# A sparse graph layer on one core: edge items worked out as a maximum and a minimum over columns sorted by sign

## The chip, the cores and the metric

The kernel runs on one core of one Trainium2 chip. The metric is the device time of one execution in microseconds (us), from the first to the last instruction of that core with what lies around it; lower is better. Engines are called by the profile's letters: PE (TensorE, matrix products), DVE (VectorE), ACT (ScalarE), POOL (GpSimd, which here issues the indirect DMAs) and SP (SyncE, which issues plain DMAs). Each engine works through its own instructions in the order in which they stand in its queue.

## What is computed

A batch of 32 entries of 512 nodes with 256 features goes through four layers on one sparse 512 x 512 matrix `adj`. Layers 0 and 3 are the same kind, layer 1 is a plain graph layer, layer 2 is attention. Cut to what matters here:

```
def gnn(h, adj, W1, b1, W2, b2, Wa, ba, Wm, bm, beta1, beta2, beta3):   # layers 0 and 3
    pre_u = h @ W1[:256];  pre_v = h @ W1[256:]
    hidden = relu(pre_u[:, :, None, :] + pre_v[:, None, :, :] + b1)     # for every pair u, v
    S = sigmoid(hidden @ W2 + b2)                                       # one number for every pair
    a_t = einsum('buv,bud->bvd', S * adj, h)
    m_t = einsum('uv,bud->bvd', adj, h) * h
    return beta1 * h + beta2 * (a_t @ Wa + ba) + beta3 * (m_t @ Wm + bm)
x = gnn(x, adj, L0...)
x = x + relu((adj @ x) @ L1_W.T + L1_b)
x = attention(x, adj, L2...)                                            # softmax over 512 neighbours
x = gnn(x, adj, L3...)
```

`S` is multiplied by `adj`, so it is needed only where `adj` is not zero: at the edges and on the diagonal. `adj` is drawn with about 1.6% of its cells filled, and its diagonal is full.

## The kernel before, in words

`Counts` (L177 on) counts the edges of each row, and one branch on that count chooses between a dense path, not taken here, and a sparse path. The sparse path lists the edges off the diagonal as 36 **items** (`Edges`): 128 edges each, one to a partition; 32 of them are own items (eight for each of the four blocks of 128 rows) and four are **panels**, the overflow of rows with more than eight edges.

The batch is worked in eight groups of four entries, and each group goes through two edge stages, one for layer 0 and one for layer 3: 16 edge stages in all. A stage has three parts.

- `pre` (L582 on) computes, for each of four entries and each of four row blocks, `pre_u` and `pre_v` by PE, adds `b1` to the first (DVE, L596), copies the second (ACT, L597), and writes the pair `puv` to a table in memory through SP (L604; `puv` has three buffers). For the self loops it also adds the two halves and takes relu, times W2, summed (DVE, L599 and L600). That is 256 `puv` pairs in all, three DVE instructions each.
- `edges` (L650 on) goes through the 36 items. For each it gathers 128 rows of 1024 numbers (four entries of 256) by an indirect DMA from POOL (L646, into one of five `rows` tiles), adds the matching tile `mine` (L731), takes relu and multiplies by W2, and sums over the 256 columns. Where the sum is left to ACT, DVE does the product in one instruction of 1024 columns (L739) and ACT sums in four (L717); otherwise DVE does product and sum in four instructions of 256 columns (L747). In 14 stages every second item up to the 31st is of the first kind, 16 of 36; in the first and in the last stage, which have spare row tiles, all 36 are. Every four items a sigmoid follows on a few columns (L614, L618, L619, L675), and POOL scatters each item's 128 x 4 results into a zeroed table of cells (L639).
- `load` reads the filled cells back as the matrix SA (L772), with which PE multiplies.

Between a group's two edge stages lies its **middle stage** (`middle_one`, L876 on): the rest of layer 0, layer 1, the softmax of layer 2 (L958 to L964, and the transposes L1003) and the `pre` of layer 3. `first` makes ready the next group's layer 0, and `last` does layer 3's products.

The order of the work is written by hand: `sparse_path` gives every piece of each of these parts a due time and `weave` issues them in that order. `behind` ties an instruction behind the one that its engine had last got two pieces of the middle stage before, so that the scheduler can't draw it ahead of that. Within these bounds a scheduler with a cost model of its own sets each engine's order at compile time.

Of the kernel before, what the change touches and what calls it, by code (L numbers as in the profile page):

```python
# [34 lines left out]
EARLY = 20  # L35
CELLS = HALF * N
ITEMS = NC * OWN + 2 * PANELS
SPARE = NC // 2 * OWN * P + LINES
GROUP = NB * D
HELD = 12  # L40

# [7 lines left out]
class Model:  # L49


    def __init__(self, ctx, tc, a):
        nc = self.nc = tc.nc
        self.tc, self.a = tc, a
        const = self.const = ctx.enter_context(tc.tile_pool(name="const", bufs=1))
        self.ident = const.tile([P, P], F32, name="ident")
        make_identity(nc, self.ident)
        self.adj = const.tile([P, NC, N], F32, name="adj")
        for c in range(NC):
            nc.sync.dma_start(self.adj[:, c, :], a["adj"][c * P : (c + 1) * P, :])  # L60
        self.g0, self.g3 = self.gnn_first("L0_gnn"), self.gnn_first("L3_gnn")
# [36 lines left out]
    def gnn_first(self, L):  # L98
        nc, a, const = self.nc, self.a, self.const
        w = {"L": L}  # L100
        w["W1"] = self.load(f"{L}_W1", [P, 2 * DC, D], a[f"{L}_W1"].rearrange("(c p) k -> p c k", p=P))
        w["b1bc"] = self.bcast(f"{L}_b1", D)
        w["W2bc"] = const.tile([P, D], F32, name=f"{L}_W2bc")
        nc.scalar.dma_start(w["W2bc"], a[f"{L}_W2"].rearrange("k o -> (k o)").partition_broadcast(P))
        w["b2"] = self.bcast(f"{L}_b2", 1)
        w["nb2"] = const.tile([P, 1], F32, name=f"{L}_nb2")
        w["bcol"] = const.tile([P, DC, 1], F32, name=f"{L}_bcol")
        if L == "L3_gnn":
# [68 lines left out]
class Counts:  # L177
# [3 lines left out]
    def __init__(self, ctx, m):  # L181
# [4 lines left out]
        with tc.tile_pool(name="c_sb", bufs=2) as sb, tc.tile_pool(name="c_ps", bufs=1, space=PSUM) as ps:  # L186
            ones = sb.tile([P, N], F32, name="c_ones", bufs=1)
            nc.vector.memset(ones, 1.0)
            count = sb.tile([P, NC], F32, name="count", bufs=1)
# [17 lines left out]
            nc.vector.tensor_reduce(half, pc.rearrange("p (h c) -> p h c", h=2), AX.X, ALU.add)  # L207
            most = sb.tile([1, 1], F32, name="most")
            nc.vector.tensor_reduce(most, half, AX.X, ALU.max)
            nc.vector.tensor_scalar(self.excess, most, float(-LINES), None, ALU.add)  # L210
# [193 lines left out]
class Group:  # L404
# [3 lines left out]
    def __init__(self, sp, w, name):  # L408
# [7 lines left out]
        self.self_s = sp.grp.tile([P, NC, NB], F32, name=f"self_s{name[0]}")  # L416

# [5 lines left out]
class Sparse:  # L423
# [3 lines left out]
    def __init__(self, ctx, m, counts, xr, outr, B):  # L427
# [16 lines left out]
        self.act, self.small, self.gath = pool("act", 1), pool("small", 2), pool("gath", 5)  # L444
# [78 lines left out]
    def big(self, dtype, n, layer=None):  # L523

        self.bigs += 1
        if layer is None:
            layer = 3 if self.bigs <= NC else 0
        return self.act.tile([P, n], dtype, name="big", tag=f"SA{layer}", bufs=NC)

    def setup(self):  # L530


        for w in (self.m.g0, self.m.g3):
            self.nc.vector.tensor_scalar(w["nb2"], w["b2"], -1.0, None, ALU.mult)
        self.zero = self.act.tile([P, GROUP], F32, name="zero", tag="hWa3")
# [30 lines left out]
    def setup_rest(self):  # L566
        yield from self.rest

# [13 lines left out]
    def pre(self, g, b, hT):  # L582
# [3 lines left out]
        for c in range(NC):  # L586
            cs = slice(c * P, (c + 1) * P)
            if c % 2 == 0:
# [7 lines left out]
            nc.vector.tensor_tensor(puv[:, 0, :], pp[:, 0:D], w["b1bc"], ALU.add)  # L596
            nc.scalar.copy(puv[:, 1, :], pp[:, D:])  # L597
            both = self.small.tile([P, D], F32, name="both", bufs=1)
            nc.vector.tensor_tensor(both, pp[:, D:], puv[:, 0, :], ALU.add)  # L599
            nc.vector.scalar_tensor_tensor(  # L600
                both, both, 0.0, w["W2bc"], ALU.max, ALU.mult, accum_out=g.self_s[:, c, b : b + 1]
            )
# [47 lines left out]
    def edges(self, g, spare=(), own_tags=()):  # L650
# [8 lines left out]
        tags = [None] * 5 + list(spare)  # L659
# [3 lines left out]
        def own_1():  # L663
            self.sigmoid_of(own)
            diag = self.counts.diag.unsqueeze(2).to_broadcast([P, NC, NB])
            nc.vector.tensor_tensor(g.self_s, g.self_s, diag, ALU.mult)
            for q in range(2):
                diagonal = g.cells[q][q * HALF : q * HALF + HALF * (N + 1), :]
                diagonal = diagonal.rearrange("(c p a) b -> p c a b", p=P, a=N + 1)[:, :, 0, :]
                self.written(g, q, nc.sync.dma_start(diagonal, g.self_s[:, 2 * q : 2 * q + 2, :]))  # L670
# [9 lines left out]
        panels = [j for j in e.order if j >= NC * OWN][: len(own_tags)]  # L680

        def fetch(n):
# [4 lines left out]
            j = e.order[n]  # L687
            c = -j if -j in mine and j >= NC * OWN else j // OWN
# [13 lines left out]
            self.fetch(rows, g, e.iv[:, j : j + 1])  # L702
# [10 lines left out]
        def sums(k, rows):  # L713

            for b in range(NB):
                part = rows[:, b * D : (b + 1) * D]
                self.behind(nc.scalar.activation(part, part, AF.Identity, accum_out=g.s[:, k, b : b + 1]))  # L717
# [7 lines left out]
        todo = [(2, lambda: self.exp_of(w, own)), (4, own_1)]  # L725
        done = 0
        for k in range(ITEMS):
            for _ in range(2 if spare and len(ready) > 2 else 1):
                put()
            rows, other = fetched.pop(k)  # L730
            self.behind(nc.vector.tensor_tensor(rows, rows, other, ALU.add))  # L731
            if k + lead < ITEMS:
                fetch(k + lead)
            if summed:
                summed.pop(0)()
            if spare or k % 2 == 1 and k < ITEMS - 3:
                by_entry = rows.rearrange("p (b d) -> p b d", b=NB)
                w2 = w["W2bc"].unsqueeze(1).to_broadcast([P, NB, D])
                nc.vector.scalar_tensor_tensor(by_entry, by_entry, 0.0, w2, ALU.max, ALU.mult)  # L739
                summed.append(lambda k=k, rows=rows: sums(k, rows))  # L740
                if spare:
                    summed.pop(0)()
            else:
                for b in range(NB):
                    part = rows[:, b * D : (b + 1) * D]
                    at = g.s[:, k, b : b + 1]
                    nc.vector.scalar_tensor_tensor(part, part, 0.0, w["W2bc"], ALU.max, ALU.mult, accum_out=at)  # L747
            if k % 4 == 3 or k >= ITEMS - 3:
                ks = slice(done, k + 1)
                near = spare or k >= ITEMS - 5  # L750
                todo.append((k + (1 if near else 3), lambda ks=ks: self.exp_of(w, g.s[:, ks, :].rearrange(flat))))
# [698 lines left out]
```

## Time and profile before

| | |
|---|---|
| median of three runs | 2982.51 us (2976.23 to 2991.17) |
| the profiled execution, its own time | 2998.45 us |
| its span, first to last instruction | 2996.8 us |
| mean clock granted to PE | 0.959 |
| PE busy | 2690.0 us, 90% |
| DVE busy | 2307.1 us, 77% |
| ACT busy | 1336.8 us, 45% |
| POOL busy | 1555.3 us, 52% |
| DMA | 677.30 MB, mean 226 GB/s |

The span is taken in a profiled execution; the 1.65 us between it and that execution's own time lies around the instructions. Busy time is what the profile shows of an engine's instructions. A PE that is shown busy isn't necessarily at its peak, and the idle time of an engine that is not the bottleneck costs nothing.

### The profile page before, as it was taken

To read this page: it belongs to the slowest core of one execution; us is meant where nothing else is said; L and a number is where in the kernel's file an instruction comes from. 1 tells how busy PE (TensorE), PEld (TensorE's weight loads), DVE (VectorE), ACT (ScalarE), POOL (GpSimd) and SP (SyncE) were. 2 spreads that over 40 slices of the span, in tenths; PEclk is the share of its full clock that TensorE was granted. 3 is DMA by queue.
4 is the path that set the end of the run, shared out by engine and by line. 5 is a ranking of instruction groups with operands and counts; after the bars stand their busy time and mean duration, and the time that the engine had idled before them with its cause. 6 is when DMAs were issued, how large, how long until landed. Compare 5 with 4: busy or idle time off the path is not lost. (4 is left out here: it accounts for less than half of the span.)

```text
span 2996.8 us, 32453 instructions
## 1 busy us (share of the span) xinstructions
PE 2690.0 (90%) x8645; PEld 1613.9 (54%) x8646; DVE 2307.1 (77%) x6035; ACT 1336.8 (45%) x4101; POOL 1555.3 (52%) x1328
## 2 busy tenths in 40 slices
PE   6367787989998999989999899989999899988998
PEld 3134344545664566546664466646565466644666
DVE  6874786889588885988778885888858896783494
ACT  3553454445344443544344443445434453453262
POOL 2662463646445673556536464466735564361183
PEclk9678998999999999999999999999999999999999
DMA  8875657796678867787677866687677866663474
GB/s 268 286 225 169 213 174 221 233 300 203 217 217 269 268 211 227 230 262 254 209 222 247 275 207 230 216 268 253 211 228 236 303 227 197 208 211 102 148 244 150
DMA packets 302143, 677.30 MB, mean 226 GB/s; under 512 B 52608, under 2 KB 170880, under 8 KB 293760
## 3 DMA queue, kind: packets, MB, share of 16 engines
q0 software_dynamic: 122688, 414.40, 42.9%
q1 hardware_dynamic: 160304, 223.52, 23.0%
q10 hardware_dynamic: 18960, 37.24, 3.4%
q8 instruction: 70, 1.15, 0.2%
q14 instruction: 121, 0.99, 0.1%
HBM read 529.02 MB, written 146.01 MB: 225 GB/s over the span
## 5 line engine op out<-in xcount | busy, mean ns | idle before, releaser
L646 POOL DMA_INDIRECT rows<-table,iv x552 | 679.0, 1230 | 795.5 <-DMA table<-puv 262.7
L639 POOL DMA_INDIRECT cells<-s,cell x576 | 697.6, 1211 | 420.6 <-DVE s L675 243.2
L731 DVE TENSOR_TENSOR rows<-rows,mine 128x1024 f32<-128x1024 f32 x552 | 666.4, 1215 | 101.4 <-DMA rows<-table,iv 72.8
L717 ACT ACTIVATE rows<-rows 128x256 f32<-128x256 f32 x1088 | 439.6, 406 | 445.4 <-DVE rows L739 396.6
L46 PE MATMUL pst<-adj,h 128*128 128x512 f32 x1024 | 452.2, 592 | 0.0
L747 DVE SCALAR_TENSOR_TENSOR rows<-rows,L_gnn_W2bc 128x256 f32<-128x256 f32 x1120 | 414.0, 417 | 1.6
L739 DVE SCALAR_TENSOR_TENSOR rows<-rows,L_gnn_W2bc 128x1024 f32<-128x1024 f32 x272 | 329.4, 1213 | 0.4
L46 PEld LDWEIGHTS pst<-adj,h 128*128 128x128 f32 x1024 | 192.8, 190 | 219.9 <-issue 217.6
L46 PE MATMUL pst<-L_gnn_Wa,hT 128*128 128x256 f32 x1024 | 248.8, 393 | 62.9 <-DMA hT<-xT 57.8
L46 PEld LDWEIGHTS pst<-L_gnn_Wa,hT 128*128 128x128 f32 x1024 | 198.9, 199 | 103.0 <-issue 59.2
L46 PE MATMUL pst<-eT,feats 128*128 128x512 f32 x512 | 237.7, 619 | 10.9 <-ACT eT L1004 10.9
L46 PE MATMUL pst<-adjT,zW 128*128 128x512 f32 x512 | 228.2, 599 | 11.6 <-ACT zW L916 9.7
L596 DVE TENSOR_TENSOR puv<-pst,bc_L_gnn_b 128x256 f32<-128x256 f32 x256 | 104.9, 416 | 162.4 <-DMA table<-puv 89.2
L597 ACT COPY puv<-pst 128x256 f32<-128x256 f32 x256 | 93.2, 371 | 288.1 <-DVE puv L596 225.9
L1061 PE MATMUL pst<-hWa,SA 128*128 128x256 f32 x896 | 220.3, 400 | 0.0
L1061 PEld LDWEIGHTS pst<-hWa,SA 128*128 128x128 f32 x896 | 213.8, 328 | 3.7 <-issue 1.7
L717 ACT ACTIVATION_READ_ACCUMULATOR rows<-rows 128x1 f32 x1088 | 204.7, 188 | 0.0
L860 ACT COPY flat<-SA 128x512 f32<-128x512 f32 x128 | 136.7, 1128 | 136.6 <-issue 62.9
L891 PE MATMUL pst<-flat,hWa 128*128 128x512 f32 x448 | 196.8, 592 | 0.0
L592 PE MATMUL pst<-w_L_gnn_W,hT 128*128 128x512 f32 x256 | 141.5, 681 | 53.9 <-ACT hT L579 36.5
L46 PEld LDWEIGHTS pst<-eT,feats 128*128 128x128 f32 x512 | 99.9, 198 | 133.2 <-issue 113.3
L46 PEld LDWEIGHTS pst<-adjT,zW 128*128 128x128 f32 x512 | 96.5, 191 | 133.4 <-issue 114.0
(176 smaller groups left out, 3984.2 us busy)
## 6 DMA issues: line engine op xcount, KB each, us to landing
table<-puv SPq DMA_DIRECT2D x256, 256.0 KB
SA<-cells POOLq DMA_DIRECT2D x64, 1024.0 KB
h<-in_x_dram SPq DMA_DIRECT2D x64, 512.0 KB
mine<-table SPq DMA_DIRECT2D x64, 512.0 KB
hT<-xT SPq DMA_DIRECT2D x36, 512.0 KB
xT<-hT ACTq DMA_DIRECT2D x32, 512.0 KB
x2T<-yT SPq DMA_DIRECT2D x32, 512.0 KB
x2s<-x ACTq DMA_DIRECT2D x64, 256.0 KB
```

Source lines behind the costliest of these rows:

```text
L46: nc.tensor.matmul(out, lhsT, rhs, start=(n == 0), stop=(n == len(pairs) - 1))
L592: nc.tensor.matmul(pp, hT[:, 0, ks], w["W1"][:, 0::DC, :], start=True, stop=False)
L596: nc.vector.tensor_tensor(puv[:, 0, :], pp[:, 0:D], w["b1bc"], ALU.add)
L639: ins = self.nc.gpsimd.indirect_dma_start(out=g.cells[half], out_offset=bass.IndirectOffsetOnAxis(ap=at, axis=0), in_=s, in_offset=None)
L646: self.nc.gpsimd.indirect_dma_start(out=rows, out_offset=None, in_=g.table, in_offset=bass.IndirectOffsetOnAxis(ap=at, axis=0))
L717: self.behind(nc.scalar.activation(part, part, AF.Identity, accum_out=g.s[:, k, b : b + 1]))
L731: self.behind(nc.vector.tensor_tensor(rows, rows, other, ALU.add))
L739: nc.vector.scalar_tensor_tensor(by_entry, by_entry, 0.0, w2, ALU.max, ALU.mult)
L747: nc.vector.scalar_tensor_tensor(part, part, 0.0, w["W2bc"], ALU.max, ALU.mult, accum_out=at)
L860: self.nc.scalar.copy(flat[:, r, :], SA[r][:, :, b])
L891: nc.tensor.matmul(pz, hWa[:, r, cs], flat[:, r, :], start=(r == 0), stop=False)
L1061: self.nc.tensor.matmul(pz[:, k * D : (k + 1) * D], SA[r][:, cs, b], hWa[:, r, :], start=(r + k == 0), stop=(alone and k == 1 and r == NC ...
```

## The change

**The arithmetic of an item.** A positive w times relu(u+v) is max(wv, -wu) + wu, and for a negative w it is min(wv, -wu) + wu. So the 256 columns are sorted by the sign of W2: 112 columns that are surely positive (maximum), 112 surely negative (minimum), and the remaining 32 in the old way (add, relu, times W2). The table then holds -w times u and w times v in the sorted columns, an item's DVE work is a maximum of 4 x 112 columns, a minimum of 4 x 112, an add of 4 x 32 and relu times W2 on 4 x 32, and the term that is missing is the sum of u over its 224 columns. That sum, `less`, is made where `puv` is made, and subtracted from an item's 128 x 4 results ahead of the sigmoid. A panel, whose `mine` is gathered row by row, subtracts `mine` itself: one more instruction of 4 x 224 columns. Where DVE makes the sum, it does so with one reduction of 4 x 256 columns in place of four sums of 256.

**Sorting on chip.** `ranks`, in `Counts`, finds each column's place and scale; the excess that the branch reads now also covers the number of positive columns (the dense path is taken if it is below 112 or above 144). `sorted_W1` multiplies W1 by that permutation with PE, for layer 0 ahead of everything else in the sparse path and for layer 3 later. b1 and W2 come in as columns, and their broadcasts are made by PE.

**Self loops as items.** The instructions L599 and L600 in `pre` go. Each edge stage has 40 steps in place of 36: when a row block's first item has had its turn, the block's self loops follow, fetched by a plain DMA from SP, with their sum always on ACT.

**Order and buffers.** The maximum, the minimum and the add of an item are each put `behind` the middle stage, where it was its one add; relu times W2 and the sum follow them by their data. There are six row tiles in place of five. EARLY, the step at which the panels' own rows are fetched in the last stage, is 24 in place of 20.

The diff, cut to its core:

```diff
-EARLY = 20
+EARLY = 24
+STEPS = ITEMS + NC
+SURE = 112
+MIXED = D - 2 * SURE
+PLACE = {0: 0, 2: 1, 1: 2, 3: 3}
...
-        self.act, self.small, self.gath = pool("act", 1), pool("small", 2), pool("gath", 5)
+        self.act, self.small, self.gath = pool("act", 1), pool("small", 2), pool("gath", 6)
...
+    def sorted_W1(self, w):
+        nc = self.nc
+        t = self.big(F32, 2048, 0)
+        W1T = t[:, 0 : 2 * N].rearrange("p (c d) -> p c d", c=DC)
+        by_v, by_u = (t[:, k * N : (k + 1) * N].rearrange("p (c d) -> p c d", c=DC) for k in (2, 3))
+        for to, scale in ((by_u, w["su"]), (by_v, w["sv"])):
+            for c in range(DC):
+                nc.vector.tensor_scalar(
+                    to[:, c, :], self.m.upto_D, w["place"][:, c, :], scale[:, c, :], ALU.is_equal, ALU.mult
+                )
+        for c in range(DC):
+            pt = self.psum()
+            for r in range(2 * DC):
+                nc.tensor.transpose(pt[:, r * P : (r + 1) * P], w["W1"][:, r, c * P : (c + 1) * P], self.m.ident)
+            nc.scalar.copy(W1T[:, c, :], pt)
+        for k, to in enumerate((by_u, by_v)):
+            pp = self.psum()
+            for d in range(DC):
+                rs = slice((DC * k + d) * P, (DC * k + d + 1) * P)
+                mm(nc, pp[:, d * D : (d + 1) * D], [(W1T[:, c, rs], to[:, c, :]) for c in range(DC)])
+            nc.scalar.copy(w["W1"][:, DC * k : DC * (k + 1), :], by_two(pp))
...
-            nc.vector.tensor_tensor(puv[:, 0, :], pp[:, 0:D], w["b1bc"], ALU.add)
+            sure = slice(0, 2 * SURE)
+            less = g.less[:, PLACE[c], b : b + 1]
+            nc.vector.scalar_tensor_tensor(
+                puv[:, 0, sure], pp[:, sure], 1.0, w["b1bc"][:, sure], ALU.mult, ALU.add, accum_out=less
+            )
+            nc.vector.tensor_tensor(puv[:, 0, 2 * SURE :], pp[:, 2 * SURE : D], w["b1bc"][:, 2 * SURE :], ALU.add)
             nc.scalar.copy(puv[:, 1, :], pp[:, D:])
-            both = self.small.tile([P, D], F32, name="both", bufs=1)
-            nc.vector.tensor_tensor(both, pp[:, D:], puv[:, 0, :], ALU.add)
-            nc.vector.scalar_tensor_tensor(
-                both, both, 0.0, w["W2bc"], ALU.max, ALU.mult, accum_out=g.self_s[:, c, b : b + 1]
-            )
...
-            self.fetch(rows, g, e.iv[:, j : j + 1])
+            if k < 0:
+                nc.sync.dma_start(rows, places[c, 1])
+            else:
+                self.fetch(rows, g, e.iv[:, j : j + 1])
...
-            rows, other = fetched.pop(k)
-            self.behind(nc.vector.tensor_tensor(rows, rows, other, ALU.add))
+            rows, other = (t.rearrange("p (b d) -> p b d", b=NB) for t in fetched.pop(n))
+            ups, downs, mixed = (slice(0, SURE), slice(SURE, 2 * SURE), slice(2 * SURE, D))
+            self.behind(nc.vector.tensor_tensor(rows[:, :, ups], rows[:, :, ups], other[:, :, ups], ALU.max))
...
-            if spare or k % 2 == 1 and k < ITEMS - 3:
-                by_entry = rows.rearrange("p (b d) -> p b d", b=NB)
-                w2 = w["W2bc"].unsqueeze(1).to_broadcast([P, NB, D])
-                nc.vector.scalar_tensor_tensor(by_entry, by_entry, 0.0, w2, ALU.max, ALU.mult)
-                summed.append(lambda k=k, rows=rows: sums(k, rows))
+            for cols, op in ((downs, ALU.min), (mixed, ALU.add)):
+                self.behind(nc.vector.tensor_tensor(rows[:, :, cols], rows[:, :, cols], other[:, :, cols], op))
+            nc.vector.scalar_tensor_tensor(rows[:, :, mixed], rows[:, :, mixed], 0.0, w2, ALU.max, ALU.mult)
+            if k >= 0 and e.order[k] >= NC * OWN:
+                sure = slice(0, 2 * SURE)
+                nc.vector.tensor_tensor(rows[:, :, sure], rows[:, :, sure], other[:, :, sure], ALU.subtract)
+            to = g.s[:, k, :] if k >= 0 else g.self_s[:, PLACE[-1 - k], :]
+            if spare or k < 0 or k % 2 == 1 and k < ITEMS - 3:
+                line = rows.rearrange("p b d -> p (b d)")
+                summed.append(lambda to=to, line=line: sums(to, line))
...
             else:
-                for b in range(NB):
-                    part = rows[:, b * D : (b + 1) * D]
-                    at = g.s[:, k, b : b + 1]
-                    nc.vector.scalar_tensor_tensor(part, part, 0.0, w["W2bc"], ALU.max, ALU.mult, accum_out=at)
+                nc.vector.tensor_reduce(to, rows, AX.X, ALU.add)
```

## The prediction

> **What bounds the kernel now.** I read the page's busy shares and slices first, then the busy time by windows, then PE's waits, then the timeline where it idles.
>
> ```profile
> PE 2690.0 (90%) x8645; PEld 1613.9 (54%) x8646; DVE 2307.1 (77%) x6035; ACT 1336.8 (45%) x4101; POOL 1555.3 (52%) x1328
> PE   6367787989998999989999899989999899988998
> DVE  6874786889588885988778885888858896783494
> ```
>
> PE bounds nearly all of it; only what shortens its idle time (2996.8 - 2690.0 = 307 us) counts. By windows it idles 154 us before 500, 125 between 500 and 2700, 27 behind. The columns below are window, length, busy PE, PEld, DVE, ACT, POOL, then PE's clock, DMA share and GB/s.
>
> ```profile
> 125.00:150.00 25.00, 0.40 (x1) 0.00 (x0) 25.00 (x60) 11.54 (x55) 18.49 (x14) 0.61 0.75 238
> 1250.00:1300.00 50.00, 44.36 (x133) 23.36 (x132) 44.06 (x122) 21.53 (x75) 34.74 (x29) 0.97 0.77 244
> 1300.00:1350.00 50.00, 39.89 (x115) 19.46 (x114) 40.27 (x136) 22.16 (x57) 24.84 (x24) 0.97 0.83 276
> 1450.00:1500.00 50.00, 50.00 (x183) 34.91 (x182) 30.98 (x95) 18.48 (x41) 25.44 (x24) 1.00 0.62 212
> ```
>
> In the first edge stage PE starves while DVE is full. Later a group takes some 350 us, with PE full in the second half and 15 to 20 us short around one softmax. PE's waits from 500 to 2700 (total, times, longest):
>
> ```profile
> PE pst L1003 <- DVE ex L964: 37.4, 22, 7.3
> PE pst L592 <- ACT hT L579: 24.0, 6, 4.9
> PE pst L46 <- ACT zW L916: 9.7, 7, 3.2
> PE pst L934 <- DVE yT L923: 8.8, 10, 1.6
> ```
>
> All those on DVE come to 77 us, on ACT to 43. But part of DVE's lateness is a DMA's: in the softmax at 1304 DVE stands in its queue behind a `puv` whose buffer is still being written out:
>
> ```profile
> 1304.43 0.42 DVE L596 TENSOR_TENSOR puv<-pst,bc_L_gnn_b 128x256 f32<-128x256 f32 x1 [2.21 <-DMA table<-puv]
> ...
> 1312.17 0.42 DVE L596 TENSOR_TENSOR puv<-pst,bc_L_gnn_b 128x256 f32<-128x256 f32 x1 [3.40 <-DMA table<-puv]
> ```
>
> **DVE's prices.** From start to start in the timeline:
>
> ```profile
> 2841.13 2.35 DVE L731 TENSOR_TENSOR rows<-rows,mine 128x1024 f32<-128x1024 f32 x2
> 2843.40 2.35 DVE L739 SCALAR_TENSOR_TENSOR rows<-rows,L_gnn_W2bc 128x1024 f32<-128x1024 f32 x2
> ...
> 1256.64 0.42 DVE L747 SCALAR_TENSOR_TENSOR rows<-rows,L_gnn_W2bc 128x256 f32<-128x256 f32 x1
> 1256.98 0.08 DVE L747 DVE_READ_ACCUMULATOR rows<-rows,L_gnn_W2bc 128x1 f32 x1
> 1256.98 0.42 DVE L747 SCALAR_TENSOR_TENSOR rows<-rows,L_gnn_W2bc 128x256 f32<-128x256 f32 x1
> ```
>
> 1024 columns cost 2.27 / 2 = 1.135 us, 256 cost 0.34, the read of the accumulator nothing. So (1.135 - 0.34) / 768 = 1.035 ns a column and 0.075 us an instruction: 448 columns 0.54, 128 0.21, 896 1.00, 224 0.31, 32 0.11.
>
> Item with ACT's sum: before 2 x 1.135 = 2.27, after 2 x 0.54 + 2 x 0.21 = 1.50; there were 296 (rows L739: 272 + 24): -228 us.
> Item summed on DVE: before 1.135 + 4 x 0.34 = 2.50, after 1.50 and a reduction of 1024. The trace has no such reduction; between one pass (1.135) and four of 256 (1.36) I take the first, one instruction with the same columns: 2.64, times 280 (1120 / 4): +38, with the other end +102.
> Panels, 64 subtractions of 896: +64. Self loops, 64 items of 1.50: +96.
> `puv`: before 3 x 0.34 = 1.02, after 0.31 + 0.11 = 0.42, times 256: -154.
> `less`: by the changed program's order 176 subtractions of at most 16 columns at 0.09: +16.
> `ranks` and two `sorted_W1`: some 40 small ones, +7.
>
> Together -161 us of 2307. So the items themselves save next to nothing (-30); what is saved is the self loops' work in `pre`. Here the Trainium skill speaks against the change: "VectorE: DVE Perf Modes", "The DRAIN you can't avoid" and "Rules for kernel authors", says that every DVE instruction pays a pipeline flush before the next, and to keep their count small; the same page puts the fixed term near 150 cycles. The change has 874 more DVE instructions in the program's order. At 150 cycles (an estimate from that page, 0.156 us) they would cost 71 us more than at my 0.075, and the saving would shrink to 90. The spacing of 0.34 us in the rows decides: I keep -161. A dependent pair side by side may add some 0.1 us; the new order mostly interleaves two items, so I take nothing, with 40 us as the bound.
>
> **The other engines.** ACT sums 64 more items, four at 0.40 us (start to start, L717): +102 us, 7% of its load. POOL's count stays, since self loops come by SP. SP gets 64 more loads of 512 KB, 34 MB or 5% of the traffic, and each must wait for a free row tile with table writes, h and hT loads queued behind it. The sixth row tile and EARLY I cost at zero: POOL waits for a tile some 0.4 us a fetch (L646 on L717 and L747, 208 us over 552), mostly beside PE's work; if anything a gain of a few us, and none of a loss. Putting minimum and add `behind` costs nothing where the add was there already; by these prices the changed order has 65 us of edge work between first and last softmax steps, over all 32 entries, where it had 58.
>
> **Where it lands, stage by stage.**
>
> (a) Setup. PE's adj transposes start at 16.56 and the first `pre` at 24.76. Now the branch waits for the ranks (some 30 more small DVE instructions in a chain through PE, and the second W2 column, fifth in ACT's DMA queue): 4 us. Then PE's queue puts W1's transposes and products ahead of adj, and ACT, behind its three DMA issues and a table load of 1.28, must copy four times 0.58 between them: 7 us more. From the first `pre` to 85 the phase also waits on DMAs (3.7 and 5.9 us on table<-puv), which run on meanwhile, so half of the 11 is absorbed: +6 (0 to +12).
>
> (b) First edge stage, 90 to 232, no PE work to hide it. DVE is never idle from 113 to 182, and everything else (puv writes, hence hT loads, hence PE) hangs behind it. It loses 36 x 0.77 - 4 x 1.0 - 4 x 1.5 = 18 us, and of the next group's `pre` 12 x 0.60 = 7. Next late are POOL (some 80 indirect DMAs at about 1.3 + 0.3 us, 128 of 142) and DMA (share 0.75 above), so I take 60%: -15 (-28 to 0).
>
> (c) 225 to 500: PE waits 37 us on DVE; -5.
>
> (d) 500 to 2700. Of DVE's 77 us I put 35 down to the DMA wait shown above (5.9 of the 6 us that one softmax loses). The remaining 42 shrink with DVE's queue: in that softmax the order shows 3.8 us less of other work (six `puv` at -0.60). I take -23, and +5 for the longer ACT queue (12% of its 43): -18 (-50 to +15).
>
> (e) The last stage. PE is busy with held-back products until 2958, then waits 5 us for SA and closes with 28 us of products. Shorter items end sooner, but only 10 us of gaps are there to be closed: -4 (-12 to +3).
>
> Sum: 6 - 15 - 5 - 18 - 4 = -36. The profiled execution took 2998.45, so 2962; its median stands at 2982.51 / 2998.45 = 0.9947 of that: **2947**. Half a per cent, the least that a measurement here can tell from no change, is 15 us; the forecast is past it.
>
> **The rivals.**
>
> *More is freed* (2900). If the DVE waits go almost whole (c -15, d -50), b gives -25 and e -10, and setup its +6, it is -94: 2904 of its own, or 2889; with a little less 2900. For it speaks a rule: "SBUF — State Buffer", "Who interferes with whom", says that a DVE instruction with two SBUF inputs blocks a GpSimd one that reads SBUF. The trace half agrees:
>
> ```profile
> 153.20 1.99 POOL L646 DMA_INDIRECT rows_more<-table,iv  x1 [1.16 <-ACT rows_more L717]
> 166.90 0.94 POOL L646 DMA_INDIRECT rows<-table,iv  x1 [0.30 <-issue]
> ```
>
> The first began just behind an L739 (153.16) and took about that instruction's remainder longer; the second began beside an L731 (166.87) and took no longer. By the rule DVE pieces of 0.54 and 0.21 in place of 1.135 would spare each indirect DMA some 0.15 us, 12 us in (b); by the second row nothing. The forecast takes nothing.
>
> *Hidden* (2982). DVE's saving falls where PE is full, and (b) meets DMA and POOL at once; setup eats the rest.
>
> *Slower: SP's queue* (3018). From 500 to 2700 SP waited 198 us for its 56 loads of `mine` (L692), 3.5 us each, since their tile had to come free. If the 64 self-loop loads wait alike, SP stands 224 us more with table writes behind it; those hold `puv`'s three buffers, DVE's queue stands behind the next `puv` as at 1304 and 1312, and PE behind that. A quarter of it exposed is +56; with 20 left of the gains, 3034 of its own: 3018. It decides once DVE's waits on table<-puv (89 us in all now) grow by more than the 36 gained.
>
> *The dense path* would be far slower, but of W2's 256 numbers, as the reference draws them, 133 are positive, the same in both layers, between 112 and 144. One in a hundred, in the last case.
>
> **How the numbers follow.** Forecast 0.50 (its own range 2915 to 2967), more 0.13, hidden 0.15, slower 0.22. Faster by over 0.5% (below 2967.6): 0.63; within: 0.15; slower: 0.22. The range leaves out about half of the more and of the slower case: 2890 to 3020.
>
> **What would show it.** DVE busy near 2146 and ACT near 1440; PE busy still about 2690; an item on DVE in pieces of 0.54 and 0.21; the first `pre` near 35; SA's first load (L772, at 229 before) near 220; PE's waits for L964 below 30 us between 500 and 2700. Wrong if pieces of 448 columns take over 0.6, if the reduction takes over 1.4, or if SP's new loads are followed by DVE waits on table<-puv.

## The result, and the profile after

The kernel after takes **3005.23 us** (median of 13 runs, 2994.54 to 3025.59), the kernel before 2983.67 beside it (13 runs, 2976.23 to 2999.01): ratio 1.0073, 95% interval 1.0052 to 1.0095. It is 22 us slower, clear of the noise; 2947, which is faster, was forecast. The profiled execution of after took 3000.39 us of its own time (span 2998.7, mean granted clock 0.956).

Busy time and the slices of PE and DVE, from the page of after:

```profile
PE 2694.2 (90%) x8720; PEld 1627.5 (54%) x8720; DVE 2115.5 (71%) x5789; ACT 1439.9 (48%) x4621; POOL 1437.3 (48%) x1332
PE   6647878989998999989999899989999899979968
DVE  6753776778587885878678785878777785763562
```

DVE lost 192 us of work, ACT gained 103, PE has nearly the same to do (2694 for 2690). PE's last slice but one had 9 tenths and has 6: the last stage has a hole. Pieces of items that take turns in DVE's timeline of after (start, length):

```profile
920.57 0.63 DVE L862 TENSOR_TENSOR rows<-rows,mine 128x448 f32<-128x448 f32 x1 [0.36 <-issue]
921.11 1.21 DVE L880 TENSOR_REDUCE s<-rows 128x4 f32<-128x1024 f32 x1
922.24 0.81 DVE L868 TENSOR_TENSOR rows<-rows,mine 128x448 f32<-128x448 f32 x2
922.98 1.08 DVE L872 TENSOR_TENSOR rows<-rows,mine 128x896 f32<-128x896 f32 x1
923.98 0.28 DVE L869 SCALAR_TENSOR_TENSOR rows<-rows,L_gnn_W2bc 128x128 f32<-128x128 f32 x1
```

From start to start it is 0.54 for the maximum, 1.13 for the reduction, 0.74 for minimum and add, 1.00 for the panel's subtraction: the prices forecast. PE's waits from 500 to 2700 in after (total, times, longest):

```profile
PE pst L682 <- ACT hT L669: 29.3, 11, 6.4
PE pst L1142 <- DVE ex L1103: 26.9, 16, 8.3
PE pst L684 <- DVE yT L1120: 24.0, 4, 7.7
PE pst L684 <- ACT hT L669: 9.8, 8, 1.3
```

The softmax's wait (L1142 on L1103, in before L1003 on L964) fell from 37.4 to 26.9, below the 30 forecast. The first, third and fourth rows are the projections of `pre`. With all their releasers PE waits 70.8 us at these two lines, where it waited 46.6 in before (and 48.9 in a second trace of before). All of PE's waits in this stretch come to 124.7 us, and to 124.9 in before: the softmax's waits shrank and the projections' grew. The windows from 500 to 2700 (length, then PE, PEld, DVE, ACT, POOL, clock, DMA share, GB/s), in before and then in after, show the same. The clock in them, 0.98 twice, is 0.983 and 0.978 to three places:

```profile
500.00:2700.00 2200.00, 2074.72 (x6733) 1241.99 (x6733) 1797.66 (x4867) 997.43 (x2986) 1216.22 (x1021) 0.98 0.73 235
500.00:2700.00 2200.00, 2076.54 (x6745) 1248.25 (x6746) 1664.88 (x4449) 1073.53 (x3367) 1135.07 (x1027) 0.98 0.76 248
```

The longest gaps of PE at the projections are 2.9 to 7.7 us in after and 3.6 to 4.9 in before. Two of about 6 us lie near 930 and 970, where one stage meets the next. DVE's timeline of after at the first, and SP's ahead of it:

```profile
930.36 0.15 DVE L1102 RECIPROCAL cols<-cols 128x1 f32<-128x1 f32 x1
934.95 0.39 DVE L688 SCALAR_TENSOR_TENSOR puv<-pst,L_gnn_b1bc 128x224 f32<-128x224 f32 x1 [4.43 <-DMA table<-puv]
935.26 0.08 DVE L688 DVE_READ_ACCUMULATOR puv<-pst,L_gnn_b1bc 128x1 f32 x1
935.26 0.48 DVE L1103 TENSOR_SCALAR ex<-ex,cols 128x512 f32<-128x512 f32 x1
```

```profile
919.38 0.34 SPq L1147 DMA_DIRECT2D h<-x2s  x1
919.94 0.40 SPq L1010 DMA_DIRECT2D hT<-xT  x1
920.49 18.90 SPq L694 DMA_DIRECT2D table<-puv  x5
```

DVE stands for 4.43 us at a `puv` whose buffer is still being written out, and the softmax's L1103 comes behind it. SP had issued that write at 920.49, just behind the loads of h and hT; it took 14.5 us until the buffer was free. A panel's own rows stand in POOL's queue meanwhile:

```profile
931.25 0.94 POOL L736 DMA_INDIRECT rows<-table,iv  x1 [2.22 <-DMA cells<-s,cell]
946.11 0.94 POOL L736 DMA_INDIRECT mine<-table,iu  x1 [13.92 <-DVE rows L872]
```

The tile comes free only with the subtraction of an earlier panel, which stands in that same DVE queue.

The last stage, in after and then in before:

```profile
2850.00:2900.00 50.00, 34.16 (x114) 23.31 (x112) 30.23 (x87) 30.32 (x138) 34.73 (x33) 0.90 0.70 226
2900.00:2950.00 50.00, 37.44 (x113) 24.18 (x114) 28.05 (x70) 16.85 (x73) 22.82 (x22) 0.83 0.66 218
2896.50:2913.60 17.10, 6.45 (x14) 4.71 (x15) 11.45 (x28) 9.21 (x42) 11.54 (x10) 0.50 0.85 235
```

```profile
2850.00:2900.00 50.00, 49.90 (x179) 36.55 (x177) 48.34 (x62) 33.46 (x152) 40.00 (x30) 1.00 0.72 242
2900.00:2950.00 50.00, 42.05 (x133) 27.82 (x134) 43.17 (x60) 27.61 (x122) 39.93 (x31) 0.90 0.62 203
```

Here DVE was busy 48 and 43 of 50 us in before and is idle 20 us of each 50 in after, and PE idles with it. (The third row of after is the stretch at half clock, taken up at the end.) PE's waits of after behind 2785:

```profile
PE pst L1212 <- DVE big L940: 16.6, 4, 13.4
PE pst L51 <- DMA hT<-x2T: 6.8, 3, 3.2
PE pst L1200 <- ACT hWa L930: 5.8, 1, 5.8
```

The 13.4 us are a wait for one product of DVE (L940) while PE's last product before it ended at 2892.3. DVE's timeline shows what the product stood behind:

```profile
2896.22 0.65 DVE L862 TENSOR_TENSOR rows<-rows,mine 128x448 f32<-128x448 f32 x1 [2.23 <-DMA rows<-table,iv]
2901.66 0.62 DVE L862 TENSOR_TENSOR rows_more<-rows_more,mine_more 128x448 f32<-128x448 f32 x1 [3.83 <-issue]
2904.96 0.68 DVE L940 TENSOR_TENSOR big<-pst,hT 128x512 f32<-128x512 f32 x1
```

Edge items stood ahead of it in DVE's queue, and DVE waited 2.23 us for gathered rows of one and 3.83 us at another, for which the trace names no releaser.

Marks along the traces (SP's store of x2 of entry 31, start of the last load of SA, end of the last instruction): before 2809.8, 2959.0, 2992.2; after 2790.3, 2938.0, 2994.6. After enters the last stage 19.5 us ahead and loads the last weights 21 ahead. In before the held-back products are done by then and 33 us of products follow; in after 57 us follow, since PE is still at the held-back ones. From the first mark to the last, PE does the same 597 products in both: busy 170.3 of 204.3 us in after and 168.0 of 182.4 in before. So the last stage is 22 us longer, and 20 of them are idle time of PE.

### The profile page after: what moved, and what is told of

It is laid out like the page before. It is cut to its first block, busy times and chain, and to the rows that moved or that the text cites. A ratio compares the mean times of both kernels' runs of the same rounds, so it can differ in the third digit from the quotient of the medians.

```text
span 2998.7 us, 33271 instructions
## 1 busy us (share of the span) xinstructions
PE 2694.2 (90%) x8720; PEld 1627.5 (54%) x8720; DVE 2115.5 (71%) x5789; ACT 1439.9 (48%) x4621; POOL 1437.3 (48%) x1332
## 3 DMA queue, kind: packets, MB, share of 16 engines
q0 software_dynamic: 122688, 414.40, 42.3%
q1 hardware_dynamic: 169520, 257.08, 25.8%
## 4 chain that ended last, share of the span: by engine, by line
PE 41%; DVE 27%; DMA 18%; issue 7%; ACT 4%; POOL 2%; ACTq 0%; SPq 0%; another core or an unknown queue 0%; DVEq 0%; POOLq 0%
PE pst L51 18%; DMA table<-puv 7%; DMA rows<-table,iv 6%; DVE rows L868 6%; DVE rows L862 5%; PE pst L1200 5%; DVE s L880 4%; PE pst L684 4%; PE pst L682 3%; PE pst L1030 3%; PE pst L1051 2%; PE pst L1073 2%; DVE rows L869 2%; PE pst L1212 2%; ACT rows L846 2%
## 5 line engine op out<-in xcount | busy, mean ns | idle before, releaser
L736 POOL DMA_INDIRECT rows<-table,iv x558 | 638.3, 1144 | 872.6 <-ACT rows L846 238.1
L729 POOL DMA_INDIRECT cells<-s,cell x576 | 643.2, 1117 | 283.9 <-issue 135.6
L846 ACT ACTIVATE rows<-rows 128x256 f32<-128x256 f32 x1344 | 541.9, 406 | 395.4 <-DVE rows L869 366.9
L868 DVE TENSOR_TENSOR rows<-rows,mine 128x448 f32<-128x448 f32 x1232 | 514.4, 445 | 0.0
L862 DVE TENSOR_TENSOR rows<-rows,mine 128x448 f32<-128x448 f32 x616 | 379.9, 617 | 120.9 <-DMA rows<-table,iv 92.8
L880 DVE TENSOR_REDUCE s<-rows 128x4 f32<-128x1024 f32 x280 | 338.1, 1207 | 2.4
L688 DVE SCALAR_TENSOR_TENSOR puv<-pst,L_gnn_b1bc 128x224 f32<-128x224 f32 x256 | 98.8, 386 | 237.3 <-DMA table<-puv 138.7
L846 ACT ACTIVATION_READ_ACCUMULATOR rows<-rows 128x1 f32 x1344 | 253.5, 189 | 4.2 <-issue 4.2
L51 PE MATMUL pst<-eT,feats 128*128 128x512 f32 x512 | 230.9, 605 | 10.7 <-ACT eT L1143 9.3
L692 ACT COPY puv<-pst 128x256 f32<-128x256 f32 x256 | 93.1, 370 | 273.6 <-DVE puv L691 168.4
L1200 PEld LDWEIGHTS pst<-hWa,SA 128*128 128x128 f32 x896 | 214.4, 328 | 10.9 <-ACT hWa L930 6.9
L682 PE MATMUL pst<-w_L_gnn_W,hT 128*128 128x512 f32 x256 | 135.4, 655 | 49.0 <-ACT hT L669 36.6
L869 DVE SCALAR_TENSOR_TENSOR rows<-rows,L_gnn_W2bc 128x128 f32<-128x128 f32 x616 | 175.4, 285 | 2.0
```

The source lines that it names most:

```text
L51: nc.tensor.matmul(out, lhsT, rhs, start=(n == 0), stop=(n == len(pairs) - 1))
L682: nc.tensor.matmul(pp, hT[:, 0, ks], w["W1"][:, 0::DC, :], start=True, stop=False)
L729: ins = self.nc.gpsimd.indirect_dma_start(out=g.cells[half], out_offset=bass.IndirectOffsetOnAxis(ap=at, axis=0), in_=s, in_offset=None)
L736: self.nc.gpsimd.indirect_dma_start(out=rows, out_offset=None, in_=g.table, in_offset=bass.IndirectOffsetOnAxis(ap=at, axis=0))
L862: self.behind(nc.vector.tensor_tensor(rows[:, :, ups], rows[:, :, ups], other[:, :, ups], ALU.max))
L868: self.behind(nc.vector.tensor_tensor(rows[:, :, cols], rows[:, :, cols], other[:, :, cols], op))
```

## The experiments

The theory that most of the runs test: what SP must wait for sets the time. It stands in the edges' loads of own rows (`mine`, L818, and the self loops', L829), table writes and the loads of h and hT come behind, and a lighter DVE meets the late write sooner. The rivals: the self loops as work; the ties; the sixth tile; `puv`'s three buffers by themselves; the panels' tile; the order of the last stage. SP's waits for a line are summed over all rows of its waits. Each ratio is to the kernel before, timed beside that run; after's own is 1.0073.

**A second trace of before** (no edit).

> The kernel before, unchanged, for a second trace of it. The first trace of before came from an execution of 2998.45 us, 15 above its median, that of after from one of 3000.39, 5 below its median, so the two traces differ by 2 us where the medians differ by 21.6. Expected: about 2984 us. If the 15 us that this execution is shorter lie before the last stage (x2 of entry 31 at about 2794 in place of 2809), the lead of 19.5 us that the first pair of traces gave after at that point is mostly an accident of one execution, and after never gained in the middle. If they lie behind it, the lead is real and all of the loss is in the last stage.

Measured 3004.91 us, where the other twelve runs of before on that chip had a median of 2996.09. x2 of entry 31 is stored at 2812.4, and the last instruction ends at 2998.7. So both traces of before are of executions 15 and 9 us above their medians, and after's is of one 5 below. Before's last stage takes 182 and 186 us, after's 204. Of the 21.6 us between the medians the last stage is then some 20. If the 15 and 5 us by which the first two executions are off their medians lie ahead of it, the lead of 19.5 us in the middle is about nothing in a typical execution (2810 - 15 against 2790 + 5). This run was to settle that; it came out long too, so it settles only the last stage.

**The self loops' rows on POOL's queue.**

```diff
-                nc.sync.dma_start(rows, places[c, 1])
+                nc.gpsimd.dma_start(rows, places[c, 1])
```

> After, with the self loops' rows fetched by POOL's queue in place of SP's. Theory of SP's queue: in after SP waits 195 us in these fetches for a row tile to come free, and what is queued behind (the table writes, the loads of h and hT) is late; without that DVE's waits for a table write that frees a puv buffer fall from 128 to about 75 us, the last stage's loads come earlier, and the time falls by 15 to 25 us against after, to about 2985 (ratio to before 1.00). Theory that the last stage's DVE and ACT order is what is late: within 5 us of after (3000 to 3010, ratio 1.006).

Ratio 1.0074 (1.0046 to 1.0102): no change from after, so not the 15 to 25 us that the theory gave. SP's longest waits in these loads, in after and then in this kernel:

```profile
SPq L829 <- DMA rows<-table,iv: 95.1, 6, 16.6
SPq L829 <- DVE s L880: 57.9, 18, 5.3
SPq L818 <- DVE s L787: 49.8, 6, 12.4
```

```profile
SPq L818 <- DVE rows L869: 143.4, 13, 25.4
SPq L818 <- DVE s L787: 80.8, 12, 12.5
```

In after L829 and L818 hold SP 268 and 127 us; with L829 gone L818 holds it 292. SP was not freed, it stands at the next load.

**No self loops among the items.**

```diff
-STEPS = ITEMS + NC
+STEPS = ITEMS
...
-                seq.append(-1 - c)
```

The diff is cut: EARLY is 20 again too, and the diagonal's weights are left out.

> After, with no self loop among the items: 36 steps a group as before, no loads of own rows for them; the diagonal's weights are left out (the sigmoid is taken of the correction alone). It prices the self loops as items with everything that they bring: DVE -96 us, ACT -72, 34 MB of loads, SP's waits. If they carry the loss (by SP's queue, by DVE or by ACT) the time falls by 25 us or more, to 2980 or below (ratio under 0.999). If the loss lies in the ordering of the items or in six row tiles, it falls by under 10 us (ratio 1.004 or more).

Ratio 1.0096 (1.0069 to 1.0123). DVE's busy time falls to 2038.2 us, ACT's to 1335.8, and the time doesn't. The work of the self loops is not the loss, nor is DVE's load what bounds. (Its trace is of the fastest of five executions, 2996.61 us at a median of 3020.48.)

**Ties on the maximum alone.**

```diff
-                self.behind(nc.vector.tensor_tensor(rows[:, :, cols], rows[:, :, cols], other[:, :, cols], op))
+                nc.vector.tensor_tensor(rows[:, :, cols], rows[:, :, cols], other[:, :, cols], op)
```

> After, with only the maximum of an item ordered behind the middle stage, as the addition was before; the minimum and the mixed columns' addition are free to be placed. If the added ties cost (DVE made to wait for work that could have been done earlier) the time falls by 10 us or more, ratio below 1.004. If they cost nothing, or protect the middle stage, it is within 5 us of after or above it (ratio 1.006 or more).

Ratio 1.1384 (1.1355 to 1.1413), clock 0.92. Its group of minima and adds (count, busy and mean ns, idle before and its releasers):

```profile
L868 DVE TENSOR_TENSOR rows<-rows,mine 128x448 f32<-128x448 f32 x1232 | 529.0, 451 | 640.7 <-DMA rows<-table,iv 491.1 <-DMA mine<-table,iu 94.5 <-DMA rows<-table 21.9
```

Untied, the scheduler puts the minima and adds ahead, where their rows haven't come, and DVE stands 641 us at them, 586 of them for gathers. Against after's ratio the ties are worth some 390 us, and without them the split item could not be used.

**Five row tiles; five `puv` buffers, or four tiles of own rows, in the room of the sixth.** All three have five tiles in turn:

```diff
-pool("gath", 6)
+pool("gath", 5)
-        tags = [None] * 6 + list(spare)
+        tags = [None] * 5 + list(spare)
```

with `bufs=5` in place of 3 for `puv` in the second, and `bufs=4` in place of 3 for `mine` in the third.

> After, with five row tiles in turn as before in place of six. One part undone. If the sixth tile only gives the fetches more room, taking it away costs 5 to 15 us (ratio 1.010 to 1.013). If it lets DVE run further ahead of the middle stage into waits that hold up the middle stage's own work, the time falls by 5 us or more (ratio below 1.006).

> After, with five row tiles and, in the room of the sixth, five puv buffers in place of three. Theory of head-of-line waits: where a stage begins, DVE reaches the bias addition into puv 4 to 9 us before the table write that frees its buffer, the softmax steps of the middle stage stand behind it, PE idles 6 us and its clock falls to half for 3 to 10 us; eight such places. With five buffers DVE's waits for table writes fall from 126 us (550 to 2700) to under 30, PE's long gaps at those places vanish, mean clock rises to 0.960 or more, and the time falls by 30 to 60 us against five tiles alone (ratio under 0.995). Theory that these waits only stand in for another bound (the writes themselves, or PE's own work): within 10 us of five tiles alone.

> After, with five row tiles and, in the room of the sixth, four tiles for own rows in place of three. In after SP stands in the own rows' loads while the tile is still read (14 us in one place, with a store of x2T and the table writes behind it), and POOL's fetch of a panel's own rows waits 80 us for the subtraction that frees the tile. If that queueing is the loss, the time falls by 15 us or more against five tiles alone (ratio about 1.000), and DVE's waits for table writes fall below 90 us. If the puv buffers are, it is within 8 us of five tiles alone.

Ratios 1.0197 (1.0173 to 1.0220), 1.0095 (1.0064 to 1.0126) and 1.0182 (1.0161 to 1.0204). The sixth tile saves 1.2%, 37 us, well over the 5 to 15 expected: DVE's waits for rows from 550 to 2700 are 54 us with six and 107 with five. DVE's waits with five tiles, then with five `puv` buffers too:

```profile
DVE rows L862 <- DMA rows<-table,iv: 107.1, 44, 6.4
DVE puv L688 <- DMA table<-puv: 89.2, 27, 9.6
```

```profile
DVE rows L862 <- DMA rows<-table,iv: 111.0, 56, 6.4
DVE puv L688 <- DMA table<-puv: 5.4, 8, 1.5
```

The waits for table writes vanish and the time falls 1.0%, some 30 us, the low end of what was expected. But the ratio was to be under 0.995 and the clock 0.960, and they are 1.0095 and 0.956: these waits cost, and they are not all. PE's longest waits at x2 (L684) stay (7.2 and then 7.4 us at most). Five buffers together with the sixth tile were not run. More tiles of own rows give nothing that can be told: 0.15%.

**Both loads of own rows on POOL's queue**, L818 and L829:

> After, with both loads of own rows (the items' shared tile and the self loop's) on POOL's queue in place of SP's, so that SP never waits for an edge's tile. Theory of SP's queue: ratio to before at or below 1.000, DVE's waits for table writes down from 126 to under 80 us. Theory of the puv buffers alone, or of POOL being held up just as long: ratio 1.005 or more.

Ratio **0.9964** (0.9947 to 0.9982): slightly faster than before. A second time:

> Both own-row loads on POOL's queue, a second time. If the first ratio of 0.9964 holds, 0.995 to 0.998; if it was a lucky call, as the two kernels built on it suggest, 0.998 to 1.000.

Ratio 0.9980 (0.9963 to 0.9996). DVE's waits for table writes (126 us in after), first and second time:

```profile
DVE puv L688 <- DMA table<-puv: 87.8, 22, 5.8
```

```profile
DVE puv L688 <- DMA table<-puv: 64.5, 18, 6.5
```

(In the second another 36 us at `puv` have no releaser shown.)

The mean clock over the timed executions is 0.959 and 0.958 (before beside them 0.959 both times), in after 0.955. The last stage takes 194 us both times.

So the edit gives back the loss, twice. But the traces do not bear out the reason that was behind it. Between 550 and 2700 SP issued after's 193 table writes a median of 0.03 us after both halves of their `puv` were done, 0.8 us at most and 10 us in all: it was not late with them. (For the loads of h and hT the trace doesn't tell it as plainly.) What grew is the time that a write takes. In the waits for which DVE stood, it was on average 8.3 us from SP's issue to DVE's start in after (14.8 at most), 6.9 in before (9.5), and 6.9 and 7.0 with both loads moved (9.5 and 12.3). The edit also takes 67 MB off the DMA queue that SP's transfers share (q1, 257.08 to 189.96 MB) and puts them on that of the gathers (q0, 414.40 to 481.52). Sharing that queue is a rival to SP's standing that no run here separates from it.

**The items' shared own rows alone on POOL's queue, in after and in before**: L818, and its counterpart L692.

> After, with only the items' shared own rows loaded by POOL's queue in place of SP's; the self loops' rows stay on SP. The self loops' rows alone on POOL changed nothing (ratio 1.0074 against after's 1.0073), both together gave 0.9964. If the shared rows' load alone is what held SP, this gives 0.996 to 0.999; if both must go, since either one leaves SP standing, it stays at 1.004 or more.

> The kernel before, with the items' shared own rows loaded by POOL's queue in place of SP's: the control for the last edit. SP stood 235 to 244 us in that load in before, 128 in after. If the load held SP just as much in before, it gains as much here (ratio 0.990 or less), and moving it says nothing of why after is slower. If it is a cost of after alone, the ratio is within 0.997 to 1.003.

Ratios 1.0141 (1.0112 to 1.0171) and 1.0049 (1.0036 to 1.0062). With L818 moved in after, L829 alone holds SP 320 us. So SP's standing in the two falls from 395 us to 292 or 320 with one load moved, and only moving both gives a gain. Moving L818 alone even costs 0.7% against after, which is not explained: PE's waits from 500 to 2700 rise from 125 to 149 us, while DVE's for table writes fall to 103. In before, SP stood 244 us in L692 and moving it off costs half a per cent; the gain isn't one that before could have had.

**Without self loops, own rows on POOL's queue.** The two edits above together.

> After with no self loops among the items (the diagonal's weights left out), and the items' shared own rows on POOL's queue: SP never stands in an edge's load. Without the self loops SP stood 244 us in that load, as much as in before (243), and the ratio was 1.0096. If SP's queue is the cause here too, the ratio falls to 0.996 or less. If the loss without self loops is another (the split item, the panels' tile), it stays at 1.004 or more, as moving this load cost before 0.005.

Ratio 0.9995 (0.9974 to 1.0015), against 1.0096 with the load on SP: again 1%, short of the 0.996 expected. But it isn't by way of `puv`; DVE's waits for table writes are 105.5 us without the move and with it

```profile
DVE puv L688 <- DMA table<-puv: 118.4, 29, 8.5
```

**The panels' tile freed early**, in after, and with both loads moved. The panels' missing term is left out, since columns of `adj` are subtracted in its place:

```diff
-                nc.vector.tensor_tensor(rows[:, :, sure], rows[:, :, sure], other[:, :, sure], ALU.subtract)
+                nc.vector.tensor_tensor(rows[:, :, sure], rows[:, :, sure], self.m.adj[:, :, sure], ALU.subtract)
```

> After, with the panels' subtraction reading the adjacency's first 224 columns in place of the panel's own rows: the same instruction at the same length, but the own rows' tile comes free one instruction group earlier (the panels' weights come out wrong by this). POOL stands up to 13.9 us (seven times, 80 us) in the fetch of a panel's own rows for this subtraction, the rows' fetches queue behind it, DVE waits for them 4 to 7 us at the end of each stage with the last of x2 behind it, and PE idles 5 to 7 us there. If the added subtraction is what makes this, POOL's wait at that line falls to the 5 us of before, PE's waits for x2 at the next projection (24 us) fall below 8, and the time falls by 20 us or more (ratio 1.000 or less). If the fetch is late for other reasons, within 8 us of after (ratio 1.005 or more).

> Both own-row loads on POOL's queue, and the panels' subtraction reading the adjacency in place of the own rows (the panels' weights come out wrong by this). If SP's queue and the tile that the subtraction holds are two causes, their gains add: 0.9964 less 0.0053 gives 0.991. If they are one chain (what frees POOL also frees SP), the ratio stays at 0.995 to 0.998.

Ratios 1.0020 (1.0004 to 1.0035) and 0.9985 (0.9966 to 1.0003). Alone it gives back 16 us, with both loads moved nothing, so the gains don't add. And it isn't as expected: POOL's wait for panels' own rows is 142 us in all, as in after (144; in before 50), now for the minimum and the add (L868). The tile is held by the whole split item, not by the subtraction alone. What gave the 16 us isn't settled; PE's waits for x2 fell only from 24.0 to 21.5.

**The last stage.** Held-back products earlier in the order, in after and with both loads moved; rows seven items ahead at the ends, with both loads moved and in before:

```diff
-            behind = end + 0.29, end + 0.45
+            behind = end + 0.22, end + 0.38
```

```diff
-LEAD_AT_ENDS = 5
+LEAD_AT_ENDS = 7
```

> After, with the last stage's held-back products put earlier in the woven order (from 0.22 to 0.38 of a stage past its end in place of 0.29 to 0.45). In after the last stage takes 204 us from the last x2 to the end, in before 182 and 186, although the last edge weights' load is issued at the same distance (148 us): PE's held-back products end 26 us after that load is issued, in before with it. If PE's order alone were late, the last stage falls to 190 us or less (time 12 us or more lower). If DVE's and SP's queues hold the products back, wherever they stand in the order, it stays above 198.

> Both own-row loads on POOL's queue, and the last stage's held-back products earlier in the order, from 0.22 to 0.38 past its end. On SP's queue as in after, the earlier order gave nothing: PE then waited 28 us for x2T, loaded by SP (14.8 at once). If SP standing in the edges' loads is what makes the last stage long, the earlier order pays once SP is free: from the last x2 to the end 188 us or less (194 with both loads moved alone), ratio to before 0.9950 or less. If DVE's order holds the products, 192 or more and no gain over 0.9964.

> Both own-row loads on POOL's queue, and rows fetched seven items ahead in place of five in the first and the last edge stage (the tiles for it are there: nine and eleven in turn). In the last stage DVE stands some 20 to 30 us for rows with the held-back products' DVE steps behind it. If that standing is what makes the last stage long, from the last x2 to the end falls from 194 to 188 us or less, and the first stage ends 2 us or more earlier. If the rows come at the rate of the DMA engines however early they are asked for (busy share 0.78 to 0.84 there), it stays within 2 us.

> The kernel before with the same seven items ahead, the control of the last edit: in before DVE is busy without a break in the last stage (48 of 50 us), so an earlier fetch gives it nothing: ratio 0.998 to 1.002, last stage within 2 us of 186. If it gains as own_lead7 does, the edit isn't about the split item.

Ratios 1.0069 (1.0043 to 1.0095), 0.9995 (0.9973 to 1.0017), 0.9974 (0.9958 to 0.9991), 0.9997 (0.9984 to 1.0010). The last stage takes 199, 202, 195 and 183 us. PE's waits there in the first and in the second:

```profile
PE pst L51 <- DMA hT<-x2T: 28.1, 6, 14.8
```

```profile
PE pst L51 <- DMA hT<-x2T: 16.2, 4, 10.8
PE pst L1212 <- DVE big L940: 11.2, 1, 11.2
```

An earlier order only exchanges the wait for DVE's product for one for hT, with both loads moved too: hT has one buffer, freed by the same product (in the second SP waited up to 10.9 us for L940), so SP isn't what makes this stage long. An earlier fetch doesn't shorten it either. With both loads moved the stage is 10 us shorter than in after (PE idles 24 us in it, for 34); the other 10 over before are not traced to one part of the change.

## Why the prediction was wrong

*DVE's sum* held: single prices to the hundredth, and in all -192 us where -161 stood. The fixed 0.075 us an instruction was the right choice against the page's 150 cycles: the maximum of 448 columns took 0.54, where 150 cycles give 0.62 (an estimate from that page's figure). *ACT* got +103 for +102. *(a)* held: the first `pre` at 34.4, forecast near 35. *(a) to (c)* together held in the trace, with some luck in the parts: x2 of entry 4 at 527.0 against 542.3, -15 for -14. At the first load of SA after was ahead by 18.7 (210.6 for 229.3) where 9 was summed, so the first edge stage gave more; from there to entry 4 it lost 3.4 where (c) said -5.

*(d)* failed: "The remaining 42 shrink with DVE's queue", -18. The waits for the softmax did shrink, by 10.5 us, but PE's waits as a whole did not (124.7 us for 124.9). The step took every other wait as it was, and put the table writes' lateness in a rival. DVE stood 126 us for table writes from 550 to 2700 where it had stood 72, and PE's waits moved to the projections of `pre` (70.8 us for 46.6). Between the stores of x2 of entries 4 and 31 the trace of after is 4 us shorter than that of before, where 18 were forecast, and this pair flatters after if the executions are off their medians in this part. The clock fell too: over the timed executions 0.955 against 0.959 in the before timed with the next runs. That would be 11 us of 2694, an estimate, if it all fell on busy time; PE's busy time rose by 4.2 us, the sorting's products among them.

*(e)* failed by most: "only 10 us of gaps are there to be closed: -4 (-12 to +3)". It took the held-back products as fixed until 2958 and asked only what could close behind them. But gaps opened among them: they depend on DVE (L940) and on hT, PE waited up to 13.4 us, and they ended later (2964) though the weights were there 21 us sooner. The stage measured 204 us for 182 and 186: some +20, of which about 10 goes with the two loads on SP. In the pair of traces the sum closes: -15 for (a) to (c), -4 for (d), +22 for (e) is the +2 by which their executions differ. The medians differ by 20 more, and no trace tells in which stage.

*The rival "SP's queue"* came nearest. Its sign was right, and so was its point of decision: DVE's waits on table<-puv grew from 89.2 to 138.7 us over the whole run, by 49.5, past 36. Its size was too big (3018 for 3005), and would have been bigger still with the 49 loads of `mine` that the trace has between 500 and 2700, in place of the 56 by which it divided. Its place was half right: not the self loops' loads alone, but own rows of either kind. Its path is not borne out: the table writes were issued on time and took longer. With both loads moved the forecast's direction comes out (0.9964 and 0.9980), but at 6 to 11 us for DVE's 192. "At zero" was wrong for the sixth tile, which saves 37 us: without it the change would have been slower still.

What stays open: how moving the two loads saves its 1%, by SP's standing or by the DMA queue that they leave. DVE's waits for table writes do not follow the time (103 us at 1.0141, 135 at 1.0020, 5 at 1.0095), so they are one part of the path at most. Open too is why the same standing of SP (243 us in before, 244 without self loops) costs 1% with the split item and nothing before. That a DVE full of edge work hid it is argued, not shown. The last 10 us of the last stage are open as well.

## What to carry to other kernels

Before pricing work off an engine that isn't the bound, list what its queue will stand at once it is early, and what stands behind: here a table write, a row tile, an own-rows tile. Sum all of the bound engine's waits before and after, since a wait that shrinks at one line can come back at another. When a transfer is waited for, tell a late issue from a long transfer before moving work between queues. Moving one of two waiting loads gave nothing here or cost time, and moving both gave 1%. Splitting one instruction into three also splits what a scheduler may move: tie each piece.

## What the hardware showed besides

- PE's clock is 1 or a half in the clock records of all 20 traces, and changes in steps of 3.4 us. What counts is the share of a step in which PE was idle, not one long gap. From 30 us on it fell 732 times, each time behind a step with at least 41% idle. It stayed at 1 behind 15184 steps, none with over 59%, and came back 712 times, each time behind a step with at most 18%. In before, the step from 953.2 to 956.6 has 2.1 us idle in 3.4, and the next one 0.50. In the window of after from 2896.50 to 2913.60 above, entered in the gap of 13.4 us, it is 0.50 for all 17 us. The Trainium skill ("TensorE: Matmul & The Clock Gate", Part 1) says that the throttled state is the default and activity releases it; the trace agrees. On average the clock lost 0.004 more than in before.
- POOL's indirect DMAs got shorter with DVE's pieces, with nothing of their own changed: the rows' from 1230 to 1144 ns and the scatters' from 1211 to 1117. That is the direction of the rule of the Trainium skill ("SBUF — State Buffer", "Who interferes with whom") weighed in the rival, at some 0.09 us each for the 0.15 worked out there. The two rows shown there disagreed; all of before's trace together is for the rule: the 240 fetches of rows that began while DVE was in an instruction with two SBUF inputs of over 0.8 us took 1.49 us on average, the 189 that began beside none 0.98.
